# Layer 3's cross attention: scores from tokens in two-bank tiles, and VectorE in source order

## The chip, the cores and the metric

The kernel runs on one core of one Trainium2 chip. TensorE (PE) multiplies matrices and transposes, VectorE (DVE) and ScalarE (ACT) read its results from PSUM (eight banks of 512 fp32 columns for each of 128 partitions), GpSimd (POOL) works on SBUF alone, and SyncE (SP) issues most of the DMAs. The metric is the device time of one execution in microseconds. Before the change it is 2157.71 us, the median of three runs (2155.54 to 2163.58).

## The reference, cut to what matters

A decoder of four layers works on x of (4, 512, 128) and a context of (4, 77, 128). Each layer adds self attention, cross attention and a feed-forward part to x, each of a layer norm of x. The change is in layer 3's cross attention:

```python
q = (query @ w_q).reshape(B, Q, 16, 64).transpose(0, 2, 1, 3)   # query: layer norm of x
k = (key @ w_k).reshape(B, 77, 16, 64).transpose(0, 2, 1, 3)    # key, value: the context
v = (value @ w_v).reshape(B, 77, 16, 64).transpose(0, 2, 1, 3)
scores = einsum('bhqd,bhkd->bhqk', q, k) * 64 ** -0.5
out = einsum('bhqk,bhkd->bhqd', softmax(scores), v)
x = x + out.transpose(0, 2, 1, 3).reshape(B, Q, 1024) @ w_o
```

Behind it stands a mixture of 32 experts, of which each token takes four, with a limit on the tokens of an expert. Its router (sigmoid of a product with `gate_w`, the four largest, their weights, a running count for the limit) is computed while the cross attention still runs on later batches.

## The kernel before, in words

All data is fp32. x, its norm `xn` and the norm's transpose `xT` stay in SBUF; a batch is four tiles of 128 tokens (TB = 4).

**Keys and values (`l3_context`, L2215; `l3_keys`, L2246).** They depend on the context alone, so they are made early, in the second group of layer 0's feed-forward part, step by step in turn with its experts (`turns`, L408). For each of eight pairs of heads (`hp`) one product gives the pair's keys of all batches (308 columns: 4 x 77), one the values; then each head's values are multiplied by its rows of w_o (16 matmuls of 64 rows; an fp32 product is two matmuls in the trace). ScalarE copies them out of PSUM, and DMAs put keys and values into DRAM. Much later `l3_keys` fills the tile `kb` with zeros on GpSimd and loads the keys into it so that a pair's two heads stand side by side, each on its own 64 partitions, with zeros in the other's (128 x 154 for a pair and batch), and `vo` with the values.

**The attention (`l3_xattn`, L2260).** There are 32 items, a batch and a pair of heads. `lagged` (L418) walks over rounds; in each round every phase handles the item that its lag says, and gives control away after each phase (a dense step: four to a round). `projections` (lag 0) makes q = Wq.T x tokens, 128 x 512, and ScalarE copies it, times 0.125. `scores` (lag 1) makes the scores of two token tiles into one PSUM bank, two banks for an item (128 x 308 each). For each of these halves VectorE takes the maximum over the keys (`sm_m`, L2301) and subtracts it (`heads`, by the helper at L442), ScalarE takes the exponential, VectorE the sum (`sm_s`, L2304) and its reciprocal (L2305), and GpSimd multiplies (L2306). `turn` (lag 3) transposes tiles of 128 of a batch's 1232 rows (16 heads x 77 keys), ScalarE copies them (`eT`), and `values` (lag 4) adds their products with `vo` up over the batch, in one bank of the tag `acc`; at a batch's last pair ScalarE copies the sum (`yT`).

**What sets the order.** `weave` (L395) takes dense steps from the attention, and after every so many of them (`every`) one step of a chain: first the norms of batches 1 to 3 and the empty rows for the experts (`empty_slots`), then for batches 0, 1 and 2 `chain5`: the sum onto x (`onto_x3`: four transposes and an addition), the norm (statistics, a reciprocal root of nine small VectorE instructions, L475 to L484, scaling on ScalarE, transposes, a copy), `router` (L585: gate products, sigmoid on ScalarE, bias), `topk`, `capped` (L696: weights, running counts, 16 small matmuls that place the tokens, `pp`) and `route_slots` (L759). A `yield` ends a step of the chain. The framework's scheduler orders each engine's instructions by its own estimate of when they are ready, with the program's order as priority (`ahead` raises it). `manual_schedule` names engines that keep the order of the source instead: in this stage GpSimd alone. GpSimd also issues the scatters of tokens to their experts (`put`): two with each item, three in the last batch, the rest after the last item.

**PSUM.** `banks(mm=5, acc=2, s=1)`: five banks for projections, scores and transposes, two for the sums, one for the chain.

Of the kernel before, what the change touches and what calls it, by code (L numbers as in the profile page):

```python
# [13 lines left out]
F32 = mybir.dt.float32  # L14
# [8 lines left out]
P = 128  # L23
# [107 lines left out]
def pack_all(inp):  # L131
# [126 lines left out]
    for n in "kvq":  # L258
        packs[f"l3_xattn.{n}"] = Pack()
        packs[f"l3_xattn.{n}"].add(n, inp["L3_xattn_w_" + n])  # L260
    packs["l3_xattn.o"] = Pack()
    packs["l3_xattn.o"].add("o", inp["L3_xattn_w_o"].reshape(8, P, D).transpose(1, 0, 2))
# [27 lines left out]
class Net:  # L290
# [58 lines left out]
    def banks(self, ctx, **tags):  # L349

        assert sum(tags.values()) <= 8
# [344 lines left out]
    def capped(self, b, W, pool, m):  # L696
# [5 lines left out]
        yield from self.router((b,), W, E, pool, m)  # L702
# [17 lines left out]
        for t in range(TB):  # L720
            self.dot(pp[:, t, :], (self.const["upper"], hit[:, t, :]), (self.ones, before[:, t, :]))

# [1492 lines left out]
    def l3_context(self, pool):  # L2215

        nc = self.nc
        Wk, Wv, Wo = (self.load("l3_xattn." + n, pool, "x3" + n) for n in "kvo")
        kd = self.away.tile([2, 64, 8, B, L], F32, name="x3_k")
# [3 lines left out]
        for hp in range(8):  # L2223
            c = slice(hp * P, hp * P + P)
            pk = self.bank("f", (P, B, L))
            self.dot(pk.rearrange("p b l -> p (b l)"), (Wk["k"][:, c], self.const["ctxT"]))
            k = pool.tile([P, B, L], F32, tag="x3kT", name="x3kT", bufs=2)
            nc.scalar.copy(k, pk)
            for h in range(2):
                nc.sync.dma_start(kd[h, :, hp], k[64 * h : 64 * h + 64])  # L2230
# [4 lines left out]
            yield  # L2235
            vo = pool.tile([L, 2, B, D], F32, tag="x3vo", name="x3vo", bufs=2)
            for h in range(2):
                po = self.bank("f", (P, B, D))
                r = slice(64 * h, 64 * h + 64)
                for b in range(B):  # L2240
                    self.dot(po[:L, b, :], (vT[r, b * L : b * L + L], Wo["o"][r, c]))
                nc.scalar.copy(vo[:, h], po[:L])
# [3 lines left out]
    def l3_keys(self, pool):  # L2246
# [3 lines left out]
        kb = pool.tile([P, 8, B, 2, L], F32, name="kb")  # L2250
        n, rest = 16 * L // P, 16 * L % P
        vo = pool.tile([P, n + 1, B, D], F32, name="vo")
        self.nc.gpsimd.memset(kb, 0.0)
        for h in range(2):
            self.nc.sync.dma_start(kb[64 * h : 64 * h + 64, :, :, h, :], kd[h])
# [4 lines left out]
    def l3_xattn(self, base, pool):  # L2260
# [5 lines left out]
        Wq = self.pack(base, "l3_xattn.q")  # L2266
# [8 lines left out]
        def projections(b, hp):  # L2275
# [7 lines left out]
        def scores(b, hp):  # L2283
# [12 lines left out]
            for i, s in enumerate(es):  # L2296
# [10 lines left out]
                if (b, hp) not in items[-2:]:  # L2307
                    self.put(2 if i and b == B - 1 else 1)
# [253 lines left out]
```

## Time and profile before

| What | Value |
|---|---|
| median of three runs | 2157.71 us (2155.54 to 2163.58) |
| profiled execution: time, span | 2141.59 us, 2139.5 us |
| busy over the span: PE, DVE, ACT, POOL | 2036.9 (95%), 1593.5 (74%), 989.7 (46%), 593.1 us (28%) |
| granted TensorE clock over the span | 0.981 |
| the attention, first projection to last addition onto x | 1899.7 to 2046.3 us of the span |
| starts of its 32 items' maxima | 1902.8 to 2026.8 us |
| the early making of keys and values | 305 to 400 us |

Times of stretches count from the span's start. A row of a group gives the line, engine, operation, the tiles (out<-in), the shape and the count; behind the bar the time that the group keeps its engine busy, the mean duration of one instruction in ns, and the idle time of the engine just before them with what ended it. Durations of neighbours on one engine overlap a little, so the timeline (start, duration, engine, line, instruction, count) gives the rate: from one start to the next. A row by stretches gives, for each engine, busy time and number of instructions, then the granted clock of TensorE (1.00 is full), the share of the DMA engines and GB/s.

### The profile page before, as it was taken

What the parts mean: (1) busy time and instruction counts of PE and PEld (TensorE: products, weight loads), DVE (VectorE), ACT (ScalarE), POOL (GpSimd) and SP (SyncE); (2) the same over time, 40 slices, a digit from 0 to 9 for tenths busy, and PEclk for the clock granted to TensorE, in tenths of its full rate; (3) what the DMA queues carried; (4) which work ended last, traced back from release to release, by engine and by line L of the source; (5) the groups of instructions that cost most, each with busy time, mean ns of one, the idle gap of its engine ahead of it and who ended that gap; (6) DMA issues with size and microseconds to landing.
All of it is one profiled execution on the core that took longest, in us unless ns stands there. A gap on an engine that the chain in (4) does not pass through costs nothing.

```text
span 2139.5 us, 27760 instructions
## 1 busy us (share of the span) xinstructions
PE 2036.9 (95%) x8798; PEld 1071.1 (50%) x8804; DVE 1593.5 (74%) x3932; ACT 989.7 (46%) x2023; POOL 593.1 (28%) x778
## 2 busy tenths in 40 slices
PE   6989999999999998999999999999999999989887
PEld 3556556554545554445444444444454444566654
DVE  6778675756675769778977788778767787589855
ACT  4556547444326453534543444344434445257642
POOL 2110101000000000433333334333333355233855
PEclk8999999999999999999999999999999999999988
DMA  6321343354452433433343344444445445503112
GB/s 174 112 71 51 101 119 91 82 132 117 107 147 79 112 96 96 94 87 101 104 120 103 96 126 122 124 107 132 128 116 138 114 107 134 126 8 97 54 53 82
DMA packets 93985, 222.56 MB, mean 104 GB/s; under 512 B 22178, under 2 KB 43106, under 8 KB 93582
## 3 DMA queue, kind: packets, MB, share of 16 engines
q1 hardware_dynamic: 90702, 218.63, 38.6%
q0 software_dynamic: 3136, 2.16, 0.4%
q8 instruction: 69, 1.13, 0.2%
q14 instruction: 78, 0.64, 0.1%
HBM read 192.55 MB, written 23.53 MB: 101 GB/s over the span
## 4 chain that ended last, share of the span: by engine, by line
PE 70%; DVE 18%; ACT 5%; issue 3%; DMA 2%; POOL 2%; SPq 0%; DVEq 0%; ACTq 0%; POOLq 0%
PE mm L431 18%; PE f L431 12%; PE mm L1874 8%; PE s L431 8%; PE acc L1039 5%; PE mm L1846 5%; PE mm L1821 4%; DVE h L442 2%; PE mm L1260 2%; DVE x L442 1%; DVE st L493 1%; PE mm L1195 1%; DVE at_m L1907 1%; PE mm L1240 1%; ACT xn L501 1%
## 5 line engine op out<-in xcount | busy, mean ns | idle before, releaser
L1782 POOL TENSOR_TENSOR gvx<-gvx 128x512 f32<-128x512 f32 (+1 forms) x256 | 262.4, 1025 | 534.9 <-DVE gvx L442 483.9
L431 PE MATMUL f<-xT,w_l_ffn 128*128 128x512 f32 (+1 forms) x700 | 332.5, 596 | 1.2 <-ACT h L1031 0.7
L1909 ACT ACTIVATE at_e<-mm,at_m 128x512 f32<-128x512 f32 x256 | 172.9, 685 | 269.1 <-DVE at_m L1907 263.5
L431 PE MATMUL mm<-w_l_ffn_qkv,xT 128*128 128x512 f32 x512 | 265.9, 606 | 3.3 <-DVE gvx L442 1.6
L1874 PE MATMUL mm<-og,w_l_ffn_o 128*128 128x512 f32 x512 | 263.2, 600 | 2.7 <-DVE og L442 1.4
L442 DVE TENSOR_TENSOR h<-h,f 128x512 f32<-128x512 f32 (+1 forms) x175 | 119.1, 683 | 121.7 <-PE f L431 94.6
L1031 ACT ACTIVATE h<-f 128x512 f32<-128x512 f32 x172 | 102.2, 596 | 210.9 <-PE f L431 186.6
L442 DVE TENSOR_TENSOR gvx<-mm,gv 128x512 f32<-128x512 f32 x256 | 173.8, 682 | 26.7 <-PE mm L431 22.8
L442 DVE TENSOR_TENSOR og<-mm,c 128x512 f32<-128x512 f32 x256 | 173.6, 681 | 22.9 <-PE mm L1874 20.9
L431 PEld LDWEIGHTS f<-xT,w_l_ffn 128*128 128x128 f32 (+1 forms) x700 | 125.7, 190 | 129.5 <-issue 107.2
L1039 PE MATMUL acc<-h,w_l_ffn 128*128 128x512 f32 x344 | 176.6, 596 | 4.8 <-DVE h L442 3.4
L1907 DVE TENSOR_REDUCE at_m<-mm 128x1 f32<-128x512 f32 x256 | 161.1, 681 | 13.6 <-PE mm L431 13.0
L1822 ACT COPY eT<-mm 128x512 f32<-128x512 f32 x256 | 137.3, 595 | 69.8 <-PE mm L1821 69.4
L1821 PEld LDWEIGHTS mm<-ident,at_e 128*128 128x128 f32 x1024 | 120.5, 142 | 66.4 <-issue 45.4
L1874 PEld LDWEIGHTS mm<-og,w_l_ffn_o 128*128 128x128 f32 x512 | 91.5, 190 | 115.0 <-issue 90.3
L1821 PE MATMUL mm<-ident,at_e 128*128 128x128 f32 x1024 | 136.0, 275 | 3.4 <-ACT at_e L1909 3.4
L431 PEld LDWEIGHTS mm<-w_l_ffn_qkv,xT 128*128 128x128 f32 x512 | 87.4, 191 | 91.5 <-issue 55.0
L431 PE MATMUL mm<-roped 64*128 64x512 f32 x512 | 130.3, 624 | 1.6 <-DVE roped L442 1.6
L1846 PE MATMUL mm<-eT,v 128*64 128x512 f32 x512 | 118.8, 599 | 2.1 <-ACT eT L1822 2.1
L442 DVE TENSOR_TENSOR h<-h,c 128x512 f32<-128x512 f32 x160 | 112.9, 711 | 4.5 <-DMA c<-l_ffn_w 1.5
L1248 ACT ACTIVATE e<-mm 128x512 f32<-128x512 f32 (+1 forms) x176 | 92.3, 553 | 45.8 <-PE mm L1244 41.8
L1202 DVE TENSOR_REDUCE m<-mm 128x1 f32<-128x512 f32 (+3 forms) x176 | 102.6, 624 | 10.1 <-PE mm L1198 9.4
(528 smaller groups left out, 3489.1 us busy)
## 6 DMA issues: line engine op xcount, KB each, us to landing
c<-gates SPq DMA_DIRECT2D x256, 256.0 KB
c<-l_ffn_w SPq DMA_DIRECT2D x96, 384.0 KB
w_l_ffn_qkv<-in_l_ffn_qkv SPq DMA_DIRECT2D x24, 640.0 KB
w_l_ffn<-in_l_ffn SPq DMA_DIRECT2D x26, 576.0 KB
w_l_ffn_o<-in_l_ffn_o SPq DMA_DIRECT2D x24, 512.0 KB
rot<-qk SPq DMA_DIRECT2D x128, 64.0 KB
d<-inverted SPq DMA_DIRECT2D x64, 128.0 KB
k_parts<-k SPq DMA_DIRECT2D x12, 384.0 KB
```

The costliest lines, as they stand in the source:

```text
L431: self.nc.tensor.matmul(out, lhsT=lhsT, rhs=rhs, start=i == 0, stop=i == len(pairs) - 1)
L442: self.nc.vector.tensor_tensor(out, a, b, op)
L1031: nc.scalar.activation(h, pg, AF.Silu)
L1039: nc.tensor.matmul(acc["t"], lhsT=W["d" + u], rhs=h, start=i == 0, stop=i == n - 1)
L1202: nc.vector.tensor_reduce(m[:, i, h0 : h0 + per], ps, AX.X, ALU.max, negate=True)
L1782: nc.gpsimd.tensor_tensor(x[:, :, :m], x[:, :, :m], x[:, :, m : 2 * m], ALU.add)
L1821: nc.tensor.transpose(p[:, j, :], es[i][hl][:, j * P : j * P + P], self.ident)
L1822: nc.scalar.copy(eT[hl][:, :, i * P : i * P + P], p)
L1846: nc.tensor.matmul(po[64 * hl : 64 * hl + 64, :], lhsT=m["v"][:, j, hl, :], rhs=eT[hl][:, j, :], start=j == 0, stop=j == TB - 1,)
L1874: nc.tensor.matmul(acc, lhsT=W["o"][:, (e - 1) * D : e * D], rhs=hs.pop(e - 1), start=e == 1, stop=e == E)
L1907: nc.vector.tensor_reduce(m, s, AX.X, ALU.max, negate=True)
L1909: nc.scalar.activation(e[:, :n], s, AF.Exp, bias=m, accum_out=den)
```

## The change

- **Scores from tokens.** Wq is packed transposed and loaded with the other three weights at the early stage. There each head's keys, already times 0.125, are multiplied by the head's 64 rows of Wq.T: 128 x 308 for each head. The two heads' results stand side by side and go to DRAM in one DMA per pair (two before). `kb` needs no zeros; four loads, one a batch, fill it. In the attention `projections` is gone, its ScalarE copy too: the stationary operand of a score matmul is the token tile itself. Its load through the ring of weight slots goes.
- **Order of the early products.** `l3_context` gives control away three times a pair (two before), and the matmuls of the values alternate between the two heads, that is, between the halves of the 128 rows, into two banks.
- **Two-bank tiles.** An item's scores are one PSUM tile over two banks (tag `two`, two tiles). Maximum, subtraction, exponential, sum, reciprocal and product are one instruction each, 616 columns wide, instead of two of 308. The exponentials go to a tile of their own (`sm_e`, three buffers); GpSimd's product writes the batch's `heads`.
- **Sums an item later.** Sum, reciprocal and product are a phase of their own (`sums`, lag 1, after `values` of lag 3); `turn` has lag 2. A round keeps four dense steps.
- **VectorE in source order** through the stage, besides GpSimd. The chain's steps are cut anew: two yields for each of the router's, two between the transposes of the sum and its addition, one after the placing matmuls. `every` is 2.3 for 2.5 in the first part and 1.0 for 0.85 in the last; the first part has 38 dense steps for 40.
- **Banks:** `banks(s=1, mm=2, acc=1, two=2)`, eight in all.

```diff
     def l3_context(self, pool):
-        Wk, Wv, Wo = (self.load("l3_xattn." + n, pool, "x3" + n) for n in "kvo")
-        kd = self.away.tile([2, 64, 8, B, L], F32, name="x3_k")
+        Wk, Wq, Wv, Wo = (self.load("l3_xattn." + n, pool, "x3" + n) for n in "kqvo")
+        kd = self.away.tile([B, P, 8, 2, L], F32, name="x3_k")
...
-            nc.scalar.copy(k, pk)
-            for h in range(2):
-                nc.sync.dma_start(kd[h, :, hp], k[64 * h : 64 * h + 64])
+            nc.scalar.mul(kT, pk, 0.125)
...
+            k = pool.tile([P, B, 2, L], F32, tag="x3kx", name="x3kx", bufs=2)
+            heads = [(h, slice(64 * h, 64 * h + 64), self.bank("f", (P, B, L))) for h in range(2)]
+            for h, r, pk in heads:
+                self.dot(pk.rearrange("p b l -> p (b l)"), (Wq["q"][r, c], kT[r]))
+            for h, r, pk in heads:
+                nc.scalar.copy(k[:, :, h, :], pk)
+            nc.sync.dma_start(
+                kd[:, :, hp].rearrange("b p h l -> p b (h l)"), k.rearrange("p b h l -> p b (h l)")
+            )
+            yield
...
-            for h in range(2):
-                po = self.bank("f", (P, B, D))
-                r = slice(64 * h, 64 * h + 64)
-                for b in range(B):
+            heads = [(h, slice(64 * h, 64 * h + 64), self.bank("f", (P, B, D))) for h in range(2)]
+            for b in range(B):
+                for h, r, po in heads:
                     self.dot(po[:L, b, :], (vT[r, b * L : b * L + L], Wo["o"][r, c]))
+            for h, r, po in heads:
                 nc.scalar.copy(vo[:, h], po[:L])
...
     def l3_keys(self, pool):
-        self.nc.gpsimd.memset(kb, 0.0)
-        for h in range(2):
-            self.nc.sync.dma_start(kb[64 * h : 64 * h + 64, :, :, h, :], kd[h])
+        for b in range(B):
+            self.nc.sync.dma_start(kb[:, b], kd[b])
...
-        def projections(b, hp):
...
         def scores(b, hp):
+            s = self.bank("two", (P, 2, 512))[:, :, : 4 * L]
+            for j in range(TB):
+                self.dot(
+                    s[:, j // 2, j % 2 * 2 * L :][:, : 2 * L],
+                    (self.tile_of(TB * b + j), kb[:, b, hp].rearrange("p h l -> p (h l)")),
+                )
...
+            nc.vector.tensor_reduce(m.rearrange("p (i n) -> p i n", i=2), s, AX.X, ALU.max)
+            self.tt(pair(t), s, pair(wide(m)), ALU.subtract)
+            nc.scalar.activation(t, t, AF.Exp)
+
+        def sums(b, hp):
...
+            nc.vector.tensor_reduce(r, t, AX.X, ALU.add)
+            nc.vector.reciprocal(r, r)
+            nc.gpsimd.tensor_tensor(made[b, "e"][:, :, 2 * hp : 2 * hp + 2, :], by_tile(t), by_tile(wide(r)), ALU.mult)
+            if (b, hp) not in items[-2:]:
+                self.put(3 if b == B - 1 else 2)
...
-        return self.lagged(items, (projections, 0), (scores, 1), (values, 4), (turn, 3))
+        return self.lagged(items, (scores, 0), (values, 3), (sums, 1), (turn, 2))
...
     def capped(self, b, W, pool, m):
-        yield from self.router((b,), W, E, pool, m)
+        for step in self.router((b,), W, E, pool, m):
+            yield
+            yield
...
             self.dot(pp[:, t, :], (self.const["upper"], hit[:, t, :]), (self.ones, before[:, t, :]))
+        yield
...
-        banks(mm=5, acc=2, s=1)
+        banks(s=1, mm=2, acc=1, two=2)
+        net.sm()
...
         def onto_x3(b):
-            net.add_columns(b, net.sums.pop(("l3_xattn", b)))
-            yield
+            t = net.turned(net.sums.pop(("l3_xattn", b)))
+            yield
+            yield
+            net.add_rows(b, t)
             yield from net.norm(b)
...
-        with tc.manual_schedule(engines={mybir.EngineType.Pool}):
-            net.weave(some(steps, 40), chained(net.norm(1), net.empty_slots(s5), net.norm(2), net.norm(3)), 2.5)
+        with tc.manual_schedule(engines={mybir.EngineType.Pool, mybir.EngineType.DVE}):
+            net.weave(some(steps, 38), chained(net.norm(1), net.empty_slots(s5), net.norm(2), net.norm(3)), 2.3)
...
-            net.weave(steps, chain5(2), 0.85, ahead=300)
+            net.weave(steps, chain5(2), 1.0, ahead=300)
```

## The prediction

> **What bounds the kernel now.** The profiled execution took 2141.59 us, of which 2139.5 are its span; the median of the runs shown is 2157.71. I work the sum against 2141.59 and put the same difference on the median. First I read the busy time by stretches, to find the stage: layer 3's cross attention runs from about 1899 (its first projection) to 2046 us (its last sum is added to x).
>
> ```profile
> core 0: us, PE busy (x) PEld busy (x) DVE busy (x) ACT busy (x) POOL busy (x), PEclk, DMA share, GB/s
> 300.00:400.00 100.00, 98.88 (x508) 63.61 (x508) 58.38 (x211) 58.76 (x111) 7.82 (x14) 1.00 0.38 101
> 1899.00:2046.00 147.00, 135.59 (x671) 91.28 (x672) 126.68 (x487) 95.73 (x193) 86.03 (x116) 0.97 0.20 61
> ```
>
> In the second stretch two engines are full, TensorE (135.6 of 147) and VectorE (126.7). The first is the stage in which the keys and values of this attention are made: TensorE alone fills it. A busy TensorE says little, so I take its rate from neighbouring starts in the timeline: a 512-column matmul follows the last by 0.43 us, a score matmul by 0.13, a transpose by 0.11. One item (a batch, two heads) has 2 + 8 + 5 + 2.5 of projection, score, transpose and value matmuls: 0.86 + 1.05 + 0.54 + 1.08 = 3.53 us. Items come every 4.1 us (first at 1902.8, last at 2031). So TensorE has about 14% of air, and VectorE is the closer bound: its idle time is 147 − 126.7 = 20.3 us, and 6.2 of that is one wait at the very end. That leaves 14.
>
> ```profile
> L2301 DVE TENSOR_REDUCE sm_m<-mm 128x4 f32<-128x308 f32 x64 | 29.0, 460 | 2.6 <-PE mm L431 2.4
> L442 DVE TENSOR_TENSOR heads<-mm,sm_m 128x308 f32<-128x308 f32 x64 | 29.0, 462 | 0.1
> L2304 DVE TENSOR_REDUCE sm_s<-heads 128x4 f32<-128x308 f32 x64 | 28.9, 464 | 2.9 <-ACT heads L2303 2.4
> L2305 DVE RECIPROCAL sm_s<-sm_s 128x4 f32<-128x4 f32 x64 | 10.4, 166 | 0.2
> L431 PE MATMUL mm<-xT,w_l_xattn_q 128*128 128x512 f32 x64 | 32.8, 596 | 1.5 <-ACT xT L2106 1.2 <-ACT eT L2318 0.3
> ```
>
> These are the groups by shape: the softmax of the 64 half items on VectorE, and the projections that go.
>
> **VectorE's instructions.** By durations a half item costs 460 + 462 + 464 + 166 ns, two of them 3.10 us. A 616-wide pass lies between the 512-wide row (682 ns) and the 1024-wide one (1238): 0.79 us, so an item would cost 3 x 0.79 + 0.17 = 2.54, a gain of 0.56, 18 us for 32 items. But durations overlap:
>
> ```profile
> 1920.92 0.45 DVE L2301 TENSOR_REDUCE sm_m<-mm 128x4 f32<-128x308 f32 x1
> 1921.29 0.85 DVE L442 TENSOR_TENSOR heads<-mm,sm_m 128x308 f32<-128x308 f32 x2
> ```
>
> The next instruction starts 0.37 us after one that takes 0.45. From start to start, idle time taken off, the 64 half items hold VectorE for 25.3 + 25.0 + 25.0 + 6.3 = 81.6 us, and all else in the stage for 44. That overlap of 0.08 is there only if the next instruction doesn't need the result; in the chain of reciprocal roots (L475 to L484) each start follows the last by 0.20 at 0.16 duration, so a dependent one starts some 0.03 after the end. In the new source order maximum, subtraction, sum of the item before, reciprocal, two of four steps depend: 0.82 + 0.71 + 0.82 + 0.09 = 2.44 us an item, 78.1 for 32. **−3.5 us**, between +3 (each pass as two of now) and −18 (the durations).
>
> [...]
>
> **TensorE and ScalarE.** 64 projection matmuls at 0.43 (27.5 us) and 32 copies of q (19 us) go; scores, transposes and values keep their number. Since VectorE is the bound, that is worth nothing by itself. It counts at the start: the first projection starts at 1899.74, the first score matmul, behind the copy, at 1901.53. Scores straight from tokens start where the projection did: **−1.8**. GpSimd's product becomes one of 616 columns, 1.4 us by the row of 308 (713 ns) doubled: nothing. Its queue stays as full: in the last batch 8 x 1.4 and some 18 scatters at 1.2 make 33 us, against VectorE's 8 x 2.44 + 11 = 30.
>
> **Source order on VectorE.** Now the scheduler moves softmax passes into waits. In source order each wait of a routing step stops all that is behind it on VectorE, the maxima that free the score banks first. The longest, from the timeline:
>
> ```profile
> 2019.15 0.37 DVE L499 SCALAR_TENSOR_TENSOR nmr<-mv,rstd 128x4 f32<-128x4 f32 x1
> 2019.56 1.65 ACT L501 ACTIVATE xn<-x,nmr,rstd 128x128 f32<-128x128 f32 x4 [0.36 <-DVE nmr L499]
> ...
> 2022.02 0.59 ACT L526 COPY xT<-s 128x512 f32<-128x512 f32 x1
> ...
> 2024.76 0.28 ACT L594 ACTIVATE sig<-s 128x128 f32<-128x128 f32 x1
> ...
> 2025.07 0.36 DVE L442 TENSOR_TENSOR sb<-sig,w_s 128x128 f32<-128x128 f32 x1 [0.31 <-ACT sig L594]
> ```
>
> From the norm's last VectorE step to the biased score 5.55 us pass. The doubled yields put four chain steps between, at 1.3 dense steps each 1.3 rounds of four: 1.3 x 2.44 = 3.2 us of cover, in the last batch 2.4. Wait: 2.35 + 2.35 + 3.15 = 7.8. The 16 matmuls that place tokens (`pp`) take some 2.2 us (0.83 for six and 1.03 for ten in the chain of waits, and the way there and back); one step covers 0.6 to 0.8: 1.4 x 3 = 4.2. A memset of GpSimd's for the empty rows, and sums behind a busy ScalarE (the sigmoid's two table loads of 1.28, the sent copies of 2.16 us): 4. Together 16 against today's 14: **+2**, between −9 (the yields cover all but 5) and +10 (each wait a scheduler's worth longer).
>
> **The tail.** From the last reciprocal (2038.18) to the end of the yT copy (2045.59) 7.4 us pass, and six value matmuls at half clock stand in it (5.27 us). With less on TensorE that backlog is smaller, the last product is 0.4 longer: **−1.5**, from 0 to −4.
>
> **Making the keys.** Wq is folded into K there, in a stretch that TensorE fills 99%. Added for each pair of heads: four matmuls of 64 rows x 308 columns, 0.257 each in a row, 1.03. Moved: the 16 matmuls of a pair's values (`po`) now alternate between the heads' row halves. What halves in turn are worth, two rows show:
>
> ```profile
> 318.83 1.60 PE L431 MATMUL f<-w_l_xattn_o,x3vT 64*77 64x128 f32 x16
> ...
> 1512.83 1.99 PE L431 MATMUL mm<-roped 64*128 64x512 f32 x8
> ```
>
> Eight 512-column matmuls on alternating halves take 1.91 to the next start where 8 x 0.43 = 3.4 would be due: 0.56 of it. So +0.58 and, for the 1.53 of the first row, −0.67: −0.7 over eight pairs. ScalarE gets 0.83 us more per pair (two 308-column copies of 0.415), and six banks instead of four go through a pool of four: +1.5. Wq's 512 KB queue on SP with the other weights, before gate loads: +0.4. **+1.2**, from −3 to +10 (no overlap of the halves: +8.2). The loads at the other end (four of 616 KB for two, without the 4.2 us memset) are due by 1899 and were issued at 1863: nothing.
>
> **Sum:** −3.5 − 1.8 + 2 − 1.5 + 1.2 = −3.6, so 2138 for the profiled execution and **2154 us** on the median.
>
> **Rivals.** (1) *The waits vanish.* TensorE and ScalarE are lighter, so the chains behind the waits run faster and the yields cover them: 5 us of idle instead of 16. −3.6 − 11 = −14.6: 2143. For it: nothing but VectorE is then near full (TensorE 2.67 of some 3.9 us an item). Against: the 5.55 us are almost all the chain's own durations. (2) *TensorE's clock falls,* the slower side:
>
> ```profile
> 2027.00:2030.50 3.50, 0.71 (x5) 0.24 (x4) 3.36 (x19) 3.19 (x7) 3.23 (x5) 0.88 0.56 182
> 2030.50:2034.00 3.50, 3.50 (x17) 3.50 (x18) 1.44 (x9) 1.40 (x3) 3.11 (x5) 0.50 0.89 272
> 2034.00:2037.50 3.50, 3.50 (x9) 1.95 (x9) 2.72 (x14) 0.00 (x0) 0.94 (x2) 0.50 0.07 25
> ```
>
> One stretch with 20% on TensorE, and the granted clock is half for some 8.5 us. If each routing chain now opens such a gap, 2.2 items of 2.67 us take 11.6 instead of 8.5 (3.1 late), the placing matmuls 3.7 instead of 2 (1.7; so it was at 2031) and the gate's chain 1.6 more: 6.4 x 3 = 19, −3.6 + 19 = +15: 2173. It decides where TensorE is below about 20% for 3 us; at 70% (2055 to 2058.5: 2.81 of 3.5, clock 1.00) it doesn't. [...] (3) *The halves don't overlap* or the banks hold TensorE up: +8.2 more, 2162. (4) *The change doesn't shorten VectorE:* a pass over two banks costs as two of now: +6.5 more, 2160.
>
> **How the numbers follow.** Forecast with (3) and (4), all within 0.5% (10.8 us, about what a measurement of this kernel can tell from no change): 0.46, of which 0.32 for the forecast itself, 0.07 each for (3) and (4). Rival (1): 0.35. Rival (2): 0.19. Range: (1) with a VectorE gain nearer to the durations reaches 2139, (2) at two to three chains 2169. Faster 0.35, same 0.46, slower 0.19.
>
> **What would show it.** VectorE's three 616-wide groups of 32 at about 0.79 us; its busy time in the stage some 122, its idle before the tail 16; the first score matmul 1.8 us earlier after the last token copy; waits of sb for ScalarE near 2.4 each and of the placing step near 1.4; the granted clock 1.00 through the stage; TensorE still full from 300 to 400. A stage shorter by 10 with less than 8 us of VectorE idle is rival (1); half clock at the routing steps is (2).

## The result: 1.1% slower, and the profile after

| | before | after |
|---|---|---|
| median, six runs each | 2160.64 us (2155.54 to 2166.96) | 2181.99 us (2174.82 to 2184.73) |
| ratio, 95% interval | | **1.0112** (1.009 to 1.0134) |
| profiled execution (before: a second profile) | 2157 us, span 2155.7 | 2182.92 us, span 2181.2 |
| first matmul of the keys to the first maximum of the attention | 1595.0 us | 1595.0 us |
| the attention, its first matmul to the start of the last addition onto x | 146.4 us | 166.2 us |
| from there to the end | 118.2 us | 116.8 us |

The prediction said 2154 us, with a range up to 2169: wrong, and on the wrong side. One plain remark on the profile that it worked with: that execution (2141.6 us) lies below all six timed runs of its own kernel. A second profile of the same kernel (`base` below), 2157 us, is typical. The two have the same attention (146.6 and 146.4 us) and differ behind it (93.2 and 118.2 us); the last section says how. Comparing the first profile with the one after would have put 24 us of the loss into a phase where there is none.

Between these two profiles 25.5 us of span differ, and 19.8 of them lie in one stage. Another 5.5 us pass before the first matmul of the keys (it starts at 299.1 and 304.6 us); two profiles of the kernel before differ there by as much (299.1 and 305.2), so the change need not be its cause. By stretches, first of the kernel before (second profile), then after (columns: stretch, length, busy time and count of PE, PEld, DVE, ACT, POOL, granted clock, DMA share, GB/s):

```profile
1891.10:2037.50 146.40, 134.35 (x673) 89.89 (x674) 125.98 (x485) 96.25 (x193) 86.22 (x117) 0.98 0.19 61
2037.50:2155.70 118.20, 83.50 (x394) 47.71 (x400) 56.55 (x137) 33.41 (x66) 48.74 (x88) 0.83 0.17 57
```

```profile
1898.20:2064.40 166.20, 125.02 (x608) 83.27 (x608) 131.67 (x363) 76.67 (x129) 81.75 (x86) 0.91 0.17 54
2064.40:2181.20 116.80, 88.07 (x394) 48.70 (x400) 56.56 (x137) 32.71 (x66) 47.99 (x87) 0.81 0.18 57
```

VectorE has 122 instructions fewer and is busy longer; TensorE's clock is lower. The groups by shape, VectorE, in the stage after:

```profile
L444 DVE TENSOR_TENSOR sm_e<-two,sm_m 128x616 f32<-128x616 f32 x32 | 25.6, 800 | 2.8
L2308 DVE TENSOR_REDUCE sm_s<-sm_e 128x8 f32<-128x616 f32 x32 | 25.1, 783 | 0.9 <-ACT sm_e L2302 0.9
L2299 DVE TENSOR_REDUCE sm_m<-two 128x8 f32<-128x616 f32 x32 | 24.9, 779 | 0.0
L2309 DVE RECIPROCAL sm_s<-sm_s 128x8 f32<-128x8 f32 x32 | 6.5, 203 | 1.1
...
L444 DVE TENSOR_TENSOR same<-same,wf 128x512 f32<-128x512 f32 x3 | 3.9, 1290 | 0.1
...
L444 DVE TENSOR_TENSOR wf<-wf,fits 128x128 f32<-128x128 f32 x3 | 2.9, 976 | 0.1
...
L444 DVE TENSOR_TENSOR sb<-sig,w_s 128x128 f32<-128x128 f32 x3 | 0.9, 292 | 12.7 <-ACT sig L596 12.7
```

The wide passes are as predicted (0.78 to 0.80 us). Two things are not: the addition to the sigmoid (`sb`) waits 12.7 us in three instances, and small instructions of the routing have grown (`same` 1290 ns, `wf` 976). The timeline of all engines shows both:

```profile
1951.12 0.11 DVE L501 SCALAR_TENSOR_TENSOR nmr<-mv,rstd 128x4 f32<-128x4 f32 x1
...
1951.27 1.65 ACT L503 ACTIVATE xn<-x,nmr,rstd 128x128 f32<-128x128 f32 x4 [1.91 <-DVE nmr L501]
...
1952.62 0.31 PEld L2321 LDWEIGHTS mm<-ident,heads 128*128 128x128 f32 x3 [0.67 <-POOL heads L2311]
1952.62 0.55 PE L2321 MATMUL mm<-ident,heads 128*128 128x128 f32 x3 [0.48 <-POOL sb L597]
...
1954.13 2.00 PE L2331 MATMUL acc<-eT,vo 128*128 128x512 f32 x2
...
1954.52 0.58 ACT L528 COPY xT<-s 128x512 f32<-128x512 f32 x1
1954.98 1.15 ACT L792 COPY sent<-xn 128x512 f32<-128x512 f32 x2
...
1956.15 1.28 ACT L596 ACT_TABLE_LOAD   x1
...
1956.44 1.34 PE L433 MATMUL s<-w_s_gate,xT 128*128 128x32 f32 x8
...
1957.82 0.28 ACT L596 ACTIVATE sig<-s 128x128 f32<-128x128 f32 x1 [0.38 <-PE s L433]
1958.13 0.29 DVE L444 TENSOR_TENSOR sb<-sig,w_s 128x128 f32<-128x128 f32 x1 [4.34 <-ACT sig L596]
...
1971.11 1.22 POOL L2311 TENSOR_TENSOR heads<-sm_e,sm_s 128x616 f32<-128x616 f32 x1 [4.42 <-DVE sm_s L2309]
1971.16 1.32 DVE L444 TENSOR_TENSOR wf<-wf,fits 128x128 f32<-128x128 f32 x1
...
1972.39 0.28 DVE L775 SCALAR_TENSOR_TENSOR code<-s,w_const 128x128 f32<-128x128 f32 x1
```

From the end of the norm's last VectorE step to `sb` it takes 6.9 us here (6.9 and 6.6 in the other two chains), 5.55 in the row that the prediction used. The norm's transposes stand on TensorE among transposes that wait for GpSimd's product, and the gate products stand behind two value matmuls (2.00). ScalarE meanwhile does copies of the routing (`sent`, 1.15) and a table load (1.28). In this chain the gate products end last: the sigmoid waits another 0.38 for them. In the other two it follows the table load without a wait (1997.48 and 2037.29), so there ScalarE's order is what ends last. VectorE has only 2.5 to 2.6 us of its own work between, so it stands 4.1 to 4.3. At 1971 an instruction that takes 0.29 elsewhere takes 1.32: it ends 0.15 after GpSimd's product.

Counted from start to start with idle time taken off, from the stage's first matmul to its last reciprocal, VectorE's work and idle time are 124.1 + 14.4 us before and 131.4 + 25.7 after. Of the work the softmax is 81.5 before, 77.0 after; all else 42.6 before, 54.4 after. That is −4.5 + 11.8 + 11.3 = +18.6, and the end behind the last reciprocal is 1.1 us longer: together the 19.8 of the stage, but for rounding.

The idle time is of two kinds. Idle stretches of over 0.15 us, the waits for other engines, come to 12.7 us before and 17.1 after; shorter ones between neighbours come to 1.7 before and 8.6 after.

### The profile page after: what moved, and what is told of

Its sections match the earlier page's. It is cut to its first block, busy times and chain, and to the rows that moved or that the text cites. A ratio compares the mean times of both kernels' runs of the same rounds, so it can differ in the third digit from the quotient of the medians.

```text
span 2181.2 us, 27427 instructions
## 1 busy us (share of the span) xinstructions
PE 2038.5 (93%) x8766; PEld 1066.4 (49%) x8772; DVE 1597.0 (73%) x3804; ACT 975.2 (45%) x1975; POOL 583.1 (27%) x745
## 4 chain that ended last, share of the span: by engine, by line
PE 69%; DVE 18%; ACT 4%; issue 3%; POOL 2%; DMA 2%; another core or an unknown queue 0%; SPq 0%; DVEq 0%; POOLq 0%; ACTq 0%
PE mm L433 17%; PE f L433 14%; PE mm L1879 8%; PE s L433 8%; PE acc L1044 5%; PE mm L1851 5%; PE mm L1826 4%; DVE h L444 2%; PE mm L1265 2%; PE mm L1200 1%; PE mm L1245 1%; DVE x L444 1%; DVE st L495 1%; DVE at_m L1912 1%; PE s L527 1%
## 5 line engine op out<-in xcount | busy, mean ns | idle before, releaser
L433 PE MATMUL f<-xT,w_l_ffn 128*128 128x512 f32 (+1 forms) x700 | 337.4, 604 | 2.0 <-DVE x L444 0.8
```

Source lines behind the costliest of these rows:

```text
L433: self.nc.tensor.matmul(out, lhsT=lhsT, rhs=rhs, start=i == 0, stop=i == len(pairs) - 1)
```

## Theories, and the experiments

**S**, the source order: VectorE stands at each sigmoid and at other links of the chains, and all behind it comes late. **G**, GpSimd's product of 1.22 us holds up small VectorE instructions, which the source order places right behind a reciprocal, where the product begins. **C**, my second rival: TensorE, a quarter lighter, idles, and its clock falls. Ratios are to the kernel before in the same group of runs, since its own median moved between groups (2156.7, 2136.3, 2153.7, 2133.3, 2135.0 us); each group ran on another chip. The stage is counted as in the first table.

| run | ratio (95%) | stage, us | clock in the stage |
|---|---|---|---|
| changed kernel | 1.0112 (1.009 to 1.0134) | 166.2 | 0.91 |
| base | 1.0003 (0.9985 to 1.002) | 146.4 | 0.98 |
| a_sched | 0.9999 (0.998 to 1.0018) | 143.6 | 0.93 |
| a_fill1 | 1.0142 (1.0113 to 1.017) | 166.2 | 0.97 |
| b_fold | 1.0065 (1.0041 to 1.0089) | 150.8 | 0.91 |
| a_place | 1.0119 (1.0092 to 1.0147) | 163.3 | 0.89 |
| a_wait | 1.0051 (1.0033 to 1.0069) | 154.9 | 0.94 |
| a_both | 1.0064 (1.0046 to 1.0081) | 157.3 | 0.89 |
| b_two | 1.002 (1.0002 to 1.0037) | 151.6 | 0.98 |
| c_steps | 1.0055 (1.0028 to 1.0082) | 157.3 | 0.89 |
| c_keys | 1.0004 (0.9981 to 1.0026) | 143.3 | 0.93 |
| d_last | 1.009 (1.0059 to 1.012) | 162.8 | 0.94 |
| d_last_wait | 1.0067 (1.0042 to 1.0093) | 160.5 | 0.89 |
| b_steps | 1.0018 (1.0 to 1.0036) | 153.2 | 0.92 |
| c_two | 0.9996 (0.9977 to 1.0015) | 149.4 | 0.99 |
| b_values | 0.9984 (0.9963 to 1.0006) | 145.0 | 0.98 |
| b_values_2 | **0.9975** (0.9959 to 0.999) | 146.4 | 0.98 |

**base**: the kernel before, no edit.

> The kernel before, once more, to have a profile of a typical execution (the one shown, 2141.6 us, lies below all of its six timed runs, 2155.5 to 2167.0). If the 14 us by which it lies low come from its attention stage or the phase behind it, this one shows a stage longer than 147 us or a last phase longer than 93 us; if they come from the 1900 us ahead, which both kernels share, those lengths stay and the stage begins some 14 us later than 1901.5. No difference in time from the kernel before: 2160, +-4.

2157.07 us. The stage is as in the first profile and begins 8.7 us earlier (1891.1); the difference is in the last phase.

**a_sched**: the changed kernel, VectorE back with the scheduler.

```diff
-        with tc.manual_schedule(engines={mybir.EngineType.Pool, mybir.EngineType.DVE}):
+        with tc.manual_schedule(engines={mybir.EngineType.Pool}):
```

> The changed kernel with VectorE in the scheduler's order again; all else of the change stays. Theory S (source order: VectorE stands still at the three sigmoids 4.1 to 4.3 us each, at the empty rows 2.3, and all behind it comes late): the idle time of VectorE in the stage falls from 25.6 to some 14 us, TensorE has fewer gaps, 2182 becomes 2160 to 2168. Theory C (clock: a TensorE that is a quarter lighter falls idle, its clock goes to half at the end of the stage and stays there through the next phase): 2178 to 2184, the clock is still at 0.5 from about 2040 to 2090. Theory G (GpSimd's 616-wide product holds up VectorE's small instructions): the same as C in time, 2175 to 2182, with the small instructions as long as now (wf 0.98, same 1.29).

0.9999: the whole loss is gone with this one word, and the stage is 2.8 us shorter than before the change. Its stretch and its groups by shape:

```profile
1897.70:2041.30 143.60, 117.40 (x608) 82.35 (x608) 119.97 (x360) 75.59 (x129) 80.20 (x83) 0.93 0.20 62
```

```profile
L2299 DVE TENSOR_REDUCE sm_m<-two 128x8 f32<-128x616 f32 x32 | 25.4, 795 | 7.0 <-PE two L433 6.8
...
L444 DVE TENSOR_TENSOR same<-same,wf 128x512 f32<-128x512 f32 x3 | 2.0, 666 | 0.0
...
L444 DVE TENSOR_TENSOR sb<-sig,w_s 128x128 f32<-128x128 f32 x3 | 1.1, 369 | 0.4 <-ACT sig L596 0.4
...
L444 DVE TENSOR_TENSOR wf<-wf,fits 128x128 f32<-128x128 f32 x3 | 0.8, 283 | 0.0
```

`sb` waits 0.4 in place of 12.7, `same` and `wf` have their short durations back. Counted as above, VectorE's work is 116.6 (softmax 72.6, all else 44.0), its idle time 18.6. So source order costs 0.0113 of 2160, some 24 us; S and G both fit, C doesn't, as the clock is 0.93 here too.

One thing in these two profiles goes beyond S. The waits over 0.15 us up to the last reciprocal, 17.1 us in source order, are 17.4 here: their sum is no smaller, they stand at other links. The longest of them, for the changed kernel and then for a_sched (us in total, times, longest):

```profile
DVE sb L444 <- ACT sig L596: 12.7, 3, 4.3
DVE none_rows L846 <- POOL none_rows L844: 2.3, 1, 2.3
DVE before L718 <- PE s L433: 1.0, 1, 1.0
```

```profile
DVE sm_m L2299 <- PE two L433: 6.8, 6, 2.5
DVE fits L729 <- PE s L433: 4.2, 3, 3.6
DVE sm_s L2308 <- ACT sm_e L2302: 3.9, 3, 2.2
```

What source order has more of is idle time of at most 0.15 us between neighbours (8.6 for 1.1) and work (softmax 77.0 for 72.6, all else 54.4 for 44.0). In source order 31 of the 32 subtractions stand right behind their own maximum, and all 32 reciprocals right behind their own sum; in a_sched one of each does, and other instructions stand between. The small instructions beside the product are the other part.

**a_fill1**: 2.5 idle matmuls of 512 columns an item, ahead of the transposes; they add work that nothing uses (`range(1)` stands for one fp32 product, two matmuls in the trace, for each transposed block).

```diff
                 t = self.mm((P, TB, P))
+                for _ in range(1):
+                    self.dot(t.rearrange("p j q -> p (j q)"), (self.ident, self.tokens(b)))
                 for j in range(TB):
```

> The changed kernel with 2.5 matmuls of 512 columns an item put ahead of the transposes, into the bank that these overwrite: 1.07 us of TensorE an item that computes nothing, in place of the 0.86 of the projections that went. Theory C: the clock stays near 1.0 at the end of the stage and behind it, the last phase takes some 95 us in place of 117, and the kernel is faster by 10 to 25 us in spite of 34 us more work on TensorE: 2157 to 2172. Theory S: nothing is gained, 2180 to 2190, since VectorE's waits stay and the sigmoid's chain has the fillers ahead of it. Theory G: 2180 to 2186.

```profile
1900.00:2066.20 166.20, 146.35 (x688) 93.62 (x688) 132.24 (x363) 75.70 (x129) 79.44 (x82) 0.97 0.17 54
```

The clock rises to 0.97, the stage takes 166.2 us as without the fillers, the time is 1.0142. **C falls:** the clock can be raised without the stage getting shorter, and in a_sched the loss goes at a clock of 0.93, so the low clock is not what costs the time. The fillers hold TensorE too, so this run alone can't tell whether they took back what the clock gave; the two runs together can.

**a_place**: chain steps only where GpSimd's product is over (numbers of steps and `every` halved with the yields).

```diff
+                for phase, lag in ((scores, 0), (values, 3), (sums, 1), (turn, 2)):
+                    if 0 <= r - lag < len(items):
+                        phase(*items[r - lag])
+                        if phase in (scores, values):
+                            yield
```

> The changed kernel, VectorE in source order as there, but steps of the routing chains are let in only between an item's subtraction and the next sum, not behind a reciprocal, where GpSimd's product (1.22 us) has just begun. The chains have as many steps a round as before. Theory G (small VectorE instructions stand until that product ends: wsum 1.20, wf 1.32, same 1.59 in place of 0.2, 0.3, 0.68): these go back to the durations that they have in the scheduler's order (wsum 0.3, wf 0.3, same 0.68), VectorE's work from the first maximum to the last addition falls from 131.6 to some 124, and the kernel takes 2172 to 2177. Theory S alone (only the waits for the sigmoid and the like cost, 26 us of idle time for 14): 2180 to 2184, the work stays at 131.

The groups show both halves of the answer:

```profile
L444 DVE TENSOR_TENSOR sb<-sig,w_s 128x128 f32<-128x128 f32 x3 | 0.9, 292 | 16.4 <-ACT sig L596 16.4
L444 DVE TENSOR_TENSOR wf<-wf,fits 128x128 f32<-128x128 f32 x3 | 0.9, 292 | 0.1
```

`wf` is short again and VectorE's work falls by 7.1 us, as G says; but the wait for the sigmoid grows from 12.7 to 16.4, all idle time up to the last reciprocal from 25.7 to 32.7, and the time is the same, 1.0119. **G is real, and taking it away in this manner gains nothing:** what VectorE finishes sooner it waits out at the next link. The edit also brings the chain's steps closer together, and so changes the cover of the waits; it doesn't show what G is worth where the cover stays.

**a_wait**: four more yields between the sigmoid and `sb`, `every` 1.2 for 1.3.

```diff
-        for step in self.router((b,), W, E, pool, m):
+        for i, step in enumerate(self.router((b,), W, E, pool, m)):
             yield
             yield
+            for _ in range(0 if i else 4):
+                yield
```

> The changed kernel with four more empty steps between the sigmoid's instruction and the addition that needs it (and 1.2 in place of 1.3 rounds' steps for each chain step, so that the chains end in their batch): some 1.3 items, 3.2 us, more of cover. Theory S: the three waits of 4.3 us shrink to about 1, idle time in the stage from 25.6 to some 16, and the kernel takes 2170 to 2175. If the wait only moves to the next link of the chain (placing matmuls, the end of the stage), 2178 to 2184.

```profile
L444 DVE TENSOR_TENSOR sb<-sig,w_s 128x128 f32<-128x128 f32 x3 | 2.4, 804 | 2.4 <-ACT sig L596 2.4
```

The wait falls from 12.7 to 2.4, the stage by 11.3 us, the ratio to 1.0051: **half of the loss was this wait.**

**a_both**: both edits, the four yields and the places.

> The edits of the two runs before together. If both costs are what the two theories say and add, 2160 to 2167: source order then costs no more than 3 to 10 us. If they hide each other, no better than the better one of the two, 2170 to 2177.

1.0064, no better than a_wait alone (1.0051): the second of the two possibilities. VectorE works 8.0 us less than in a_wait and stands 9.5 us longer, for the scores (9.9 us in place of 3.8) and the placing matmuls (5.2) above all. So the places gain nothing with the long wait for the sigmoid or without it; the work that they save comes back as other waits.

**d_last, d_last_wait**: the changed kernel, and a_wait, with the last `weave` in a block of its own in which GpSimd alone keeps the source's order.

```diff
+        with tc.manual_schedule(engines={mybir.EngineType.Pool}):
             net.weave(steps, chain5(2), 1.0, ahead=300)
```

> The changed kernel with VectorE in the scheduler's order in the last batch's part alone (from the third routing chain on); source order before that. If the source order costs most in the last batch, where the routing's last instructions stand ahead of the last softmax sums, the stage falls from 166 to some 150 us and the ratio to the kernel before from 1.0112 to about 1.004. If the cost is the same in each of the three chains (the sigmoid's wait of 4.3 us each, and small instructions held up), a third of 25 us comes back, 1.007 to 1.008.

> The same with four more steps of cover for the sigmoid in every batch, as in a_wait (1.0051). If the rest of the cost is in the last batch, 0.999 to 1.002, no worse than the scheduler's order throughout (0.9999); if it is spread, 1.003 to 1.005.

1.009 and 1.0067: the last batch has no more than its share. d_last_wait came out above both of its branches, and not below a_wait (the intervals of the two overlap): with the scheduler's order in the last batch nothing was gained on top. The other half of the loss is spread. From the first reciprocal to that of item 8, where no sigmoid is yet waited for, source order takes 30.9 us, the scheduler's 22.3 (before the change 22.2), though the scheduler also defers some of that work. Which of its many moves are worth what stays open.

**b_fold, b_two, c_steps**: parts alone. b_fold is the kernel before with the folded Wq and the value rows in turn only; b_two the kernel before with wide tiles, late sums and the banks that they leave only (two in place of five for projections and transposes, one for the sums); c_steps is a_sched with the routing steps uncut, as before.

The core of b_fold, of b_two and of c_steps (the last against a_sched):

```diff
-        return self.lagged(items, (projections, 0), (scores, 1), (values, 4), (turn, 3))
+        return self.lagged(items, (scores, 0), (values, 3), (turn, 2))
```

```diff
-        return self.lagged(items, (projections, 0), (scores, 1), (values, 4), (turn, 3))
+        return self.lagged(items, (projections, 0), (scores, 1), (values, 4), (sums, 2), (turn, 3))
```

```diff
-        for step in self.router((b,), W, E, pool, m):
-            yield
-            yield
+        yield from self.router((b,), W, E, pool, m)
...
-            net.weave(steps, chain5(2), 1.0, ahead=300)
+            net.weave(steps, chain5(2), 0.85, ahead=300)
```

> The kernel before with the folded projection alone: keys made as in the changed kernel, scores from the tokens; half tiles, the scheduler's order on VectorE and the routing steps as before (yields in proportion to the three phases that are left). It isolates the lighter TensorE and the making of the keys. Theory C: slower than before by 8 to 20 us (2168 to 2180), with half clock at the end of the stage. Theory S: 2152 to 2160, the gain of an earlier start and a shorter end without the waits. The making of the keys (300 to 410 us) costs by the prediction 1.2 us, by the profile of the changed kernel at most some 5 us, of which 3 come back: the first score matmul then starts no later than the first projection did.

> The kernel before with the two-bank tiles and the sums an item later alone: projections and keys as before, the scheduler's order and the routing steps as before (steps in proportion to the five phases). By the kernel with the fold and the scheduler's order, whose VectorE work from the first maximum to the last addition was 119.5 us for 124.9, the wide passes gain 5 us of VectorE; without the keys' 4 to 8 us this would be 2150 to 2155, if TensorE (3.5 us an item with its projections, two banks for them and the turned heads) lets it. If two banks for both are too few, TensorE waits for ScalarE's copies and it takes 2160 to 2175.

> The changed kernel with VectorE in the scheduler's order and the routing steps as before the change too (no doubled steps, the turned sum added in one step, 0.85 in the last batch): fold, wide tiles and sums an item later are left of the change. If the doubled steps are of use to the scheduler as well, by more cover, this is slower than the kernel with the scheduler's order alone (ratio 0.9999): 1.001 to 1.004. If they only push the end of the routing back, it is faster: 0.996 to 0.999, with the placing step's last wait (3.6 us before the last reciprocal) shorter.

1.0065, 1.002 and 1.0055: the fold alone is a loss, the wide tiles alone barely one, and a_sched loses without the doubled steps. b_fold fits what C expected (a clock of 0.91, 1.0065), but the waits for the placing matmuls (2.2, 2.5, 3.6 us) may explain it as well, and a_fill1 speaks against the clock. Only 4.4 us of its loss are in the stage; from the keys' first matmul to the attention's it took 1598.3 us in its one profile, 1592.0 in base. In b_two VectorE's softmax is 7.9 us shorter (73.6 for 81.5), but VectorE stands 12.7 us for exponentials, 2.4 in base. In c_steps GpSimd's timeline shows a price of the order that I hadn't in view:

```profile
2026.82 1.24 POOL L2308 TENSOR_TENSOR heads<-sm_e,sm_s 128x616 f32<-128x616 f32 x1
2030.81 0.20 POOL L597 MEMSET sb<- 128x32 f32 x1 [2.76 <-DVE hit L645]
2040.84 1.01 POOL L803 DMA_INDIRECT slots<-sent,to  x1 [9.83 <-DVE sent L799]
...
2044.41 2.40 POOL L2308 TENSOR_TENSOR heads<-sm_e,sm_s 128x616 f32<-128x616 f32 x2
```

Scatters that need the routing's result stand ahead of the last two products in GpSimd's fixed order; it stands 9.8 us for them, and all behind it: the last addition onto x waits 14.0 us, 5.0 in a_sched. In a_sched, with the doubled steps, the last product ran at 2033, ahead of such scatters.

**b_steps, c_two**: the doubled steps without the fold; c_two has the wide tiles too. Both have the value rows in turn. Their common edit to the kernel before:

```diff
-        yield from self.router((b,), W, E, pool, m)
+        for step in self.router((b,), W, E, pool, m):
+            yield
+            yield
```

> The kernel before with the doubled routing steps of the change and the value rows' matmuls in turn; projections, half tiles and the scheduler's order as before. If the doubled steps help the scheduler here as they do with the fold (12 us there, nearly all of it at the end of the stage, where scatters that wait for the routing stood ahead of GpSimd's last products), 0.990 to 0.996. If that stand is only there with the fold (in the kernel before the last reciprocal is 8 us ahead of the sum's addition, as in the better of the two), 0.998, the values' part.

> b_two (wide tiles, sums an item later, projections and scheduler's order as before: 1.002) with the doubled routing steps and the value rows' matmuls in turn. If the doubled steps are worth here what they are with the fold, 0.994 to 0.997: then this beats both kernels. If not, 1.000.

1.0018 and 0.9996. Without the fold the doubled steps gain nothing. That their worth in a_sched was where those scatters came to stand is what the two timelines suggest; no run moves the scatters alone.

**c_keys, b_values, b_values_2**: the early products. c_keys is a_sched with the folding matmuls cut into 154 columns, heads in turn; b_values is the kernel before with the value rows' matmuls in turn, the lines of the change and nothing else of it; b_values_2 repeats it. The diff of c_keys against a_sched, then that of b_values against the kernel before:

```diff
-                self.dot(pk.rearrange("p b l -> p (b l)"), (Wq["q"][r, c], kT[r]))
+                self.dot(pk[:, :2].rearrange("p b l -> p (b l)"), (Wq["q"][r, c], kT[r, : 2 * L]))
+            for h, r, pk in heads:
+                self.dot(pk[:, 2:].rearrange("p b l -> p (b l)"), (Wq["q"][r, c], kT[r, 2 * L :]))
```

```diff
-            for h in range(2):
-                po = self.bank("f", (P, B, D))
-                r = slice(64 * h, 64 * h + 64)
-                for b in range(B):
+            heads = [(h, slice(64 * h, 64 * h + 64), self.bank("f", (P, B, D))) for h in range(2)]
+            for b in range(B):
+                for h, r, po in heads:
                     self.dot(po[:L, b, :], (vT[r, b * L : b * L + L], Wo["o"][r, c]))
-                nc.scalar.copy(vo[:, h], po[:L])
+            for h, r, po in heads:
+                nc.scalar.copy(vo[:, h], po[:L])
```

> The changed kernel with VectorE in the scheduler's order, and with the folding matmuls of a pair of heads cut into 154 columns, the two row halves in turn. In the changed kernel the 32 records of these hold TensorE for 7.08 us, 0.221 each, where the prediction had 4.6; seen one by one, other matmuls stand between the two heads, so that the halves seldom run side by side. If that is the reason, 0.14 to 0.17 a 308 columns' worth, 4.5 to 5.5 us, and 1.5 to 2.5 us less up to the first score matmul: ratio 0.9988 to the kernel before. If the halves don't overlap in this form at all, 7 us or more and a ratio of 1.000 to 1.001.

> The kernel before with one thing of the change: the value rows' matmuls (16 a pair of heads) take the two heads' row halves in turn. In the profiles of the changed kernel they hold TensorE for 9.69 us, before it for 12.91: a gain of 3.2 us in a stretch that TensorE fills, ratio 0.9985. If the two banks that are now taken at once hold the dense work up, 1.000.

> The kernel of b_values once more, to narrow its interval. From the keys' first matmul to the attention's first it took 1586.8 us in the one profile there is, for 1592.0 (and 1587.6 and 1586.9 in two other kernels with the same edit). If that is the edit and nothing is lost behind it, a ratio of 0.9975 to 0.999; if the gain goes into waits behind it, 1.000.

Groups by shape in that stretch, after the change and then before it:

```profile
L433 PE MATMUL f<-w_l_xattn_o,x3vT 64*77 64x128 f32 x128 | 10.6, 277 | 0.0
L433 PE MATMUL f<-x3kT,w_l_xattn_q 64*128 64x308 f32 x32 | 8.6, 471 | 0.0
```

```profile
L431 PE MATMUL f<-w_l_xattn_o,x3vT 64*77 64x128 f32 x128 | 13.7, 279 | 0.0
```

From start to start the value rows take 9.7 us after and 12.9 before; the folding takes 7.1. The timeline after the change tells why so much:

```profile
308.28 0.79 PE L433 MATMUL f<-x3kT,w_l_xattn_q 64*128 64x308 f32 x4
309.00 0.70 PE L433 MATMUL f<-xT,w_l_ffn 128*128 128x512 f32 x1
...
321.27 0.78 PE L433 MATMUL f<-x3kT,w_l_xattn_q 64*128 64x308 f32 x2
321.98 0.44 PE L527 MATMUL s<-ident,xn 128*128 128x128 f32 x2
322.35 0.78 PE L433 MATMUL f<-x3kT,w_l_xattn_q 64*128 64x308 f32 x2
```

Both heads side by side (x4) take 0.72 us to the next start; one head alone (x2) takes 0.71 as well. The halves do run together, where nothing stands between; three of eight pairs were parted. c_keys (7.07 us for 64 matmuls of half the width, 1.0004) gained nothing: a pair in one run took 0.73 there, and some runs were parted still. b_values gains: 0.9984 (0.9963 to 1.0006, not clear of no change) and, repeated, 0.9975 (0.9959 to 0.999). It beats both kernels, by 0.25% of the kernel before, with a few moved lines; the attention takes what it took (145.0 and 146.4 us), the stretch from the keys to the first maximum is shorter (1589.9 and 1591.7 us for 1595.0).

## Why the prediction was wrong, step by step

- **VectorE's passes, −3.5:** right in sign, too large. The prediction counted the gap behind a dependent instruction with the pass; so counted the softmax takes 80.9 us for 82.5, −1.6 (without these gaps 77.0 for 81.5). With the scheduler's order it is 73.0. Rival 4 (two banks cost two passes) is out by the durations: one pass is 0.78 to 0.80. But its two halves took no more than 0.78 to 0.79 from start to start, and only where other instructions stand between does the wide pass get below that (0.71 to 0.72 in a_sched), so in source order it comes near.
- **Source order, +2: the step that failed.** By a_sched source order costs some 24 us, far outside of the bounds of −9 and +10. The step counted waits alone: 16 us against 14 before, and left all else on VectorE at its 44 us. The waits over 0.15 us are 17.1 against 12.7, so their 16 came out nearly right, but by luck: the sigmoid's are 12.7 for 7.8 (cover 3.2 and 2.4 assumed, 2.5 to 2.6 there; chain 5.55 assumed, 6.6 to 6.9 there), those of the placing step 1.0 for 4.2. The term that it put at nothing is the larger: VectorE's work outside the softmax grew by 11.8 us, of which 6.7 go when small instructions no longer stand beside GpSimd's product (a_place), and the short idle times between its dependent neighbours by 4.0. Together 15.8 us, of 19.8 that the stage grew by. Waits and work are not separate prices either: covering the sigmoid gained half of the loss (a_wait), shortening the work gained nothing (a_place, a_both).
- **The variant beside it.** Against the kernel before, the same change in the scheduler's order wins 7.5 us of VectorE's work and loses 4.2 to idleness (a_sched, up to the last reciprocal). The prediction didn't price it, so the cost of the order alone stayed out of sight.
- **Earlier start −1.8 and keys +1.2:** the sum, −0.6, is within what the profiles can tell. From the keys' first matmul to the first maximum, 1595.0 after and 1595.0 before; over eleven profiles with the fold 1597.8 on average (1591 to 1602), over three without fold and without the value rows in turn 1596.7. The keys' parts were mis-sized: folding 7.1 for 4.6, value rows −3.2 for −5.4. Set against the forecast's −0.7, halves that don't overlap would also have been 8.9 more and not 8.2.
- **Tail −1.5:** wrong in sign, 9.1 us for 8.0 from the last reciprocal to the last addition. The last sums stand behind the routing's comparisons, and the last matmuls run at half clock (0.50 from 2050 to 2064); in the first profile six value matmuls do (0.50 from 2030.5 to 2037.5), the last four run at 1.00.
- **Rival 1** (the waits vanish): the opposite. **Rival 2** (the clock): it did fall, as I had priced it, to 0.50 from 2050 to 2064; raised by a_fill1, the stage's length stayed. The right symptom, the wrong cause; its 2173 is nearer to 2182 than the forecast by luck. Its bound of 20% on TensorE, my estimate from one row (0.71 of 3.5 us, from 2027, then 0.50), isn't settled either: the row that it gives as 70% is 80% (2.81 of 3.5 us), a stretch of the first profile with 23% (0.81 of 3.5, from 2048) kept the clock at 1.00, and one of the changed kernel with 30% (1.22 of 4.0, from 2036) was followed by 0.50. **Rival 3** (the halves don't overlap): they do (two heads in 0.72 us, one in 0.71), at a price in and out (0.2 us each way).
- **What bounds the kernel:** the last item's maximum starts at 2026.8, not at 2031, so that items came every 4.0 us and TensorE had 12% of air, not 14; nothing in the sum hangs on it.
- Of what I had named as signs, the idle time before the tail (26 for 16) and the waits of `sb` (4.3 for 2.4) gave the failed step away at once.

## What to carry to other kernels

Price a switch to a fixed order as a change of every wait on that engine, for each link where it waits for chains on other engines that are *not* fixed, and set it against the rest of the change in the old order, not against the old kernel. Count with it what the scheduler's order hides: the gap between dependent neighbours (here short idle times of 8.6 us in place of 1.1), and small instructions beside another engine's long one (1.32 us in place of 0.29 beside a product of 1.22). Here shorter work ahead of such a wait was worth nothing (1.0119 for 1.0112) and more cover was (1.0051). A low clock beside idle time can be its consequence (here idle matmuls raised it from 0.91 to 0.97, and the stage took 166.2 us as without them): fill it and look at the length before you believe it.

## What the hardware showed that I hadn't expected

- **VectorE beside GpSimd.** While the product ran, `wf`, `same` and `wsum` stood until about its end (1.32, 1.59 and 1.20 us for 0.29, 0.68 and 0.17), but MAX8 took its usual 0.18 at 1961.13, beside a product from 1961.12, and maxima from PSUM their usual 0.79 (at 1951.15, product from 1951.35). What decides which of them stand, no run shows.
- **Going over to 64-row matmuls and back.** Two 308-column matmuls of 64 rows take 0.71 us where those of 128 rows take 0.52. In c_keys's runs of half the width the first and the last take 0.23 and 0.22 to the next start, those between 0.13: 0.1 on the way in, 0.1 on the way out. The neighbours pay the same once more: a 512-column matmul of 128 rows takes 0.52 to the start of such a run and 0.53 behind one, 0.43 elsewhere. Together the price here is 0.2 each way, 0.4 for going over and back; what TensorE does in that time, no run shows.
- **Standstills in the last phase.** In the second profile of the kernel before, TensorE stood four times for 3.8 to 5.4 us, VectorE and ScalarE with it for the most part, and their waits end with a release that the profile doesn't name. Two of these stretches, VectorE's conversions at 2046 apart:

```profile
2046.00:2049.00 3.00, 0.00 (x0) 0.00 (x0) 1.36 (x2) 0.06 (x1) 2.63 (x5) 0.82 0.02 1
...
2116.80:2119.70 2.90, 0.00 (x0) 0.00 (x0) 0.00 (x0) 0.60 (x1) 1.33 (x4) 0.99 0.02 0
```

Behind them this profile's clock is 0.50 (2050 to 2060), 0.57 (2095 to 2100) and 0.50 (2120 to 2125). The phase takes 106 to 120 us in the profiles that have such standstills, of either kernel and of the edits, and 92 to 98 in those without. They come and go with the group of runs, as the median of the kernel before does (2154 and 2157 us, or 2133 to 2136), and each group had a chip of its own: all seven profiles from two chips have a stop of TensorE of 4.1 us or more in this phase, all nine from the other three none above 2.7. With one group on each, chip and time of the runs can't be told apart; for the runs of the result and for the first profile the record names no chip. What they wait for stays open.
